# Row edges computed as corrections on a few columns, beside a convolution that now runs over all 1024 columns

## The chip, the cores and the metric

The kernel runs on one core of one Trainium2 chip. Five engines work side by side, each with its own instruction stream: TensorE (PE in the profile, its weight loads PEld), VectorE (DVE), ScalarE (ACT), GpSimd (POOL) and SyncE (SP), which here issues nearly all transfers. The metric is the device time of one execution in microseconds; lower is better. Three runs of the kernel before took 474.04, 475.82 and 476.01 us, so the median is 475.82 us. A run of the profiler on the same kernel has a span of 475.5 us from its first to its last instruction.

## The reference

Four linear layers along a row of 1024 columns with 64 channels, for 128 samples, and a residual. Each layer scales its input channels by a style vector of the sample and its output channels by a normalising factor; the kernel folds the four layers into one convolution per sample wherever the row's ends do not matter.

```python
def _layer(x, style, w, b, mw, mb, typ):
    s = style @ mw.T + mb
    weight = SCALE * w * s[:, None, :, None]
    demod = lax.rsqrt(jnp.sum(weight * weight, axis=(2, 3)) + EPS)
    weight = weight * demod[:, :, None, None]
    if typ == 'same':
        out = jax.vmap(_conv_same)(x, weight) + b[None, :, None]
    elif typ == 'upsample':
        out = jax.vmap(_conv_up)(x, weight.transpose(0, 2, 1, 3)) + b[None, :, None]
        out = _blur(out, 2.0 * blur_k, (1, 1))
    elif typ == 'downsample':
        xb = _blur(x, blur_k, (2, 2))
        out = jax.vmap(_conv_down)(xb, weight) + b[None, :, None]
    return out
out = x                                   # (128, 64, 1024) float32
for i, typ in enumerate(('same', 'upsample', 'same', 'downsample')):
    out = _layer(out, style, weights[i], biases[i], mod_w[i], mod_b[i], typ)
x = x + out
```

Near the two ends of a row the zero padding of each single layer counts, so the one folded convolution is not what the four layers give there; this concerns the first three and the last three columns.

## The kernel before

**Tiling.** The 128 samples are 32 quads of four (`NQ` = 32, index `q`). The partitions hold 64 channels of one sample above 64 channels of another, and a quad has two such pairs in the free dimension. A row is split into three phase planes (every third column). `NB` = 340 is the number of output columns that the folded convolution makes per plane, 1020 in all, of which the host keeps 1018; the first and last three columns of the output come from elsewhere.

**One product.** For a quad the convolution is done as five products (`conv0` to `conv4`, all through `product`, L792) of summed input planes (tiles `T04`, `T12`, `T3`, made by `in04`, `in1`, `in2`, `in3` from `X` and from the half sums `G`) with summed weights. A product is three tap groups times four 64x64 quadrants of the array, twelve calls of `nc.tensor.matmul`, each with `NB` moving columns; float32 leaves two records for each call, so a product shows as 24 records of L803. `conv3`, `conv1`, `conv2`, `conv0` write the PSUM tile `psA` of their quad (pool `ps_conv`, two buffers, so quad `q+1` takes the buffer of quad `q-1`); `conv4` writes the single tile `Y`. VectorE carries partial results between them (`sum1`, `sum2`), ScalarE scales the three finished planes into the tile `o` (`outputs`, pool `opool`, two buffers), and SP stores them.

**The chain of weights.** In the same loop the folded weights of later quads are made by small matmuls: `stage1` (L428), `stage2` (L506, L589; ScalarE copies its result out as `R`, GpSimd adds two sums in `r_sums`, L638), `stage3` (L621). `share` (L506 into `psA`) puts part of stage 2 into the unused columns of `psA` from `NB + 4` on.

**A turn.** `turn_of(q)` (L1483) writes the instructions of all engines in order by hand for q = 4 to 28; `early_turn` does it for q = 0 to 3 and a straight piece of code from L1560 on for the last three quads. The order of the parts on TensorE in a turn is: stage 2 of quad q+2, `conv2(q)`, the first part of stage 3 (which opens the `psA` buffer for quad q+1), `conv4(q)`, the rest of stage 3, `conv3(q+1)`, stage 1, `conv0(q)`, more of stage 1, `share`, the slot (below), `conv1(q+1)`.

**The row ends.** `x_ends` brings eight columns of each end of each row (one zero column and seven of x) into `Xe`. They go through the four layers exactly, for all 128 samples at once, in five slots: `ends0` in turn 10, the two halves of `ends1` in turns 14 and 15, `ends2` in turn 19 (all four into `Y`) and `ends3` in turn 28 (into a tile of its own, `psE`). Each slot is three taps times four quadrants, 12 calls or 24 records of L1044 (`ends_matmul`), directly ahead of `conv1`. Upper and lower array rows hold the two row ends, and a matmul has 64 samples times up to eight columns. After a slot VectorE scales the result (`rest0` to `rest3`); the steps between slots (`setup_x`, `setup0`, `add0`, `setup1`, `rest1_bias`, `rest1_edges`, `setup3`, `add2`, `blur_side`) lie one by one in other turns through the table `SIDE`, in VectorE's order just behind `in_g2`. GpSimd zeroes the borders of the tiles in `zeros` (turn 6). At the end `rest3_bias` (L1158) adds bias and x and issues two stores of 96 KB on SP.

Of the kernel before, what the change touches and what calls it, by code (L numbers as in the profile page):

```python
# [54 lines left out]
C = 64  # L55
K = 3
# [7 lines left out]
def kernel(  # L64
# [74 lines left out]
    Xs = [const.tile([P, 2, NXC], F32, name=f"X{i}") for i in range(NX)]  # L139
# [24 lines left out]
    Xe = const.tile([P, B, 8], F32, name="Xe")  # L164
# [9 lines left out]
    NB = 340  # L174
# [578 lines left out]
    def g_tile(q):  # L753
        if q not in Gs:
            Gs[q] = gpool.tile([P, 2, 3 * PL], F32, tag="G", name=f"G{q}")
        return Xs[q % NX], Gs[q]
# [136 lines left out]
    WIDE = 6  # L893
    ends_ps = {}

    def slot(matmuls, n, ps, wide=WIDE):
        matmuls(ps)
        ends_ps[0] = ps, max(n, wide)

    def last(i, n, j):  # L900
        ps, w = ends_ps[0]
        return ps[i][:, : n * w].rearrange("c (b j) -> c b j", b=n)[:, :, :j]


# [81 lines left out]
    Xm = const.tile([P, B, 8], F32, name="Xm")  # L986
    Xs0 = [Xm[:, :HB], Xm[:, HB:]]
    a0, c0, a2, c2 = (const.tile([P, HB], F32, name=n) for n in ("a0", "c0", "a2", "c2"))
    g1 = const.tile([P, 6, C], F32, name="g1")

    Ye = [const.tile([P, HB, 8], F32, name=f"Ye{s}") for s in range(2)]
    Ue = [const.tile([P, HB, 11], F32, name=f"Ue{s}") for s in range(2)]
    Ve = [const.tile([P, HB, 12], F32, name=f"Ve{s}") for s in range(2)]
    Oe = const.tile([P, B, 3], F32, name="Oe")

    def zeros():
        for t in Ye:
            nc_g.memset(t[:, :, 0:1], 0.0)
            nc_g.memset(t[:, :, 7:8], 0.0)
        for t in Ue:  # L1000
            nc_g.memset(t[:, :, 0:1], 0.0)
            nc_g.memset(t[:, :, 10:11], 0.0)
        for t in Ve:
            nc_g.memset(t[:, :, 0:2], 0.0)
            nc_g.memset(t[:, :, 10:12], 0.0)
        nc_g.memset(g1, 0.0)

    def spread(t, n):

        return t[:, :, None].to_broadcast([P, t.shape[1], n])  # L1010
# [7 lines left out]
    def setup_x(h):  # L1018
        bs = slice(h * HB, (h + 1) * HB)
        nc_v.tensor_tensor(Xm[:, bs], Xe[:, bs], spread(sc[:, 0, bs], 8), op=ALU.mult)  # L1020

    def setup0():

        for rows, bs in ((T, slice(0, HB)), (Bo, slice(HB, B))):
            nc_v.tensor_mul(a0[rows], dm[rows, 1, bs], dm[rows, 0, bs])
            nc_v.tensor_copy(c0[rows], c0f[rows, bs])
# [4 lines left out]
    def setup3():  # L1031
        for rows, bs in ((T, slice(0, HB)), (Bo, slice(HB, B))):
            nc_v.tensor_copy(a2[rows], Da[rows, bs])
            nc_v.tensor_copy(c2[rows], c2f[rows, bs])

    def ends_matmul(ps, n, taps, weight, moving, wide=WIDE):
        for i in reversed(range(taps)):
            first = i == taps - 1
            w = max(n, wide)
            m = w if first else n  # L1040
            for r, rows in enumerate(HALF):
                for c, cols in enumerate(HALF):
                    dst = ps[r][cols, : HB * w].rearrange("c (b j) -> c b j", j=w)
                    nc.tensor.matmul(  # L1044
                        dst[:, :, :m],
                        weight(i, r, c)[rows],
                        moving(i, r, c, m)[rows],
                        start=first,
                        stop=(i == 0),
                        skip_group_check=True,  # L1050
                    )

    def ends0(ps):

        ends_matmul(
# [11 lines left out]

    def ends1(part):

        n = 5 - part  # L1070


        def weight(i, r, c):
# [648 lines left out]
```

## Time and profile before

| What | Value |
|---|---|
| Runs of the kernel | 474.04, 475.82, 476.01 us |
| Span of the profiled execution | 475.5 us |
| PE busy / records | 469.7 us (99%) / 11932 |
| VectorE busy | 417.3 us (88%) |
| ScalarE busy | 312.0 us (66%) |
| GpSimd busy | 165.8 us (35%) |
| DMA | 70.71 MB, mean 149 GB/s |
| VectorE's waits at `sum2` for TensorE (L712 behind L803) | 26.9 us in 26 waits |
| Mean granted TensorE clock | 0.998 |

How to read it: the page gives for each engine the time in which at least one of its instructions ran. Records of TensorE overlap (four quadrants run side by side, and a record goes on for some time after the next has begun), so the busy time of a group of matmuls is not what it costs. What a group costs is read from the timeline, as the difference between the start of its first record and the start of the first record of the next group. In a line of the timeline the columns are start and length in microseconds, the engine, the line of the kernel, the operation, the tiles written and read, the shape and the number of records; idle time before it, with what ended it, stands in brackets.

### The profile page before, as it was taken

The page shows a single profiled execution, that of the slowest core. Times are in us where ns is not written, and L with a number is a line of the kernel's source. Part 1 is how long each engine was busy: PE and PEld are TensorE (multiplying, and loading weights), DVE is VectorE, ACT ScalarE, POOL GpSimd, SP SyncE. Part 2 cuts the span into 40 slices and gives each one's busy share as a digit, 9 for nine tenths or more (in the row PEclk, how much of TensorE's full clock was granted, in tenths as well). Part 3 has the DMA queues.
Part 4 walks back from the last instruction along what each step waited for, and adds up shares of the span by engine and source line. Part 5 has one row for each costly group of instructions (what it writes and reads, how often), then busy time and mean ns, then how long its engine had stood idle before and what let it go on. Part 6 is the DMA issues. An engine that isn't in the chain of part 4 may idle for free.

```text
span 475.5 us, 26771 instructions
## 1 busy us (share of the span) xinstructions
PE 469.7 (99%) x11932; PEld 349.5 (74%) x11932; DVE 417.3 (88%) x694; ACT 312.0 (66%) x711; POOL 165.8 (35%) x200
## 2 busy tenths in 40 slices
PE   9999999999999999999999999999999999999996
PEld 6987788777678876677776677766788787876653
DVE  3889998879989998899979899979998999999896
ACT  4565657577766676766667666667666777766464
POOL 3634033664444342233432233422333423243200
PEclk9999999999999999999999999999999999999999
DMA  5237456535445554345544454543555544455225
GB/s 176 71 115 224 150 151 180 152 113 177 139 145 166 166 166 136 123 150 169 163 150 126 130 168 152 178 124 121 152 164 169 164 145 147 148 152 161 80 91 193
DMA packets 52707, 70.71 MB, mean 149 GB/s; under 512 B 6000, under 2 KB 50672, under 8 KB 52592
## 3 DMA queue, kind: packets, MB, share of 16 engines
q1 hardware_dynamic: 52368, 68.78, 46.3%
q8 instruction: 93, 1.52, 1.4%
q10 hardware_dynamic: 224, 0.22, 0.1%
q14 instruction: 22, 0.18, 0.1%
HBM read 35.36 MB, written 33.62 MB: 145 GB/s over the span
## 4 chain that ended last, share of the span: by engine, by line
PE 99%; DVE 0%; ACT 0%; issue 0%
PE psA L803 47%; PE Y L803 12%; PE psR L506 9%; PE psW L621 7%; PE psA L621 7%; PE psS L428 6%; PE psR L589 5%; PE psA L506 2%; PE Y L1044 2%; PE Y L183 1%; PE Y L379 1%; PE psM L220 0%; PE psE L1044 0%; PE Y L255 0%; DVE o L882 0%; PE psM L255 0%
## 5 line engine op out<-in xcount | busy, mean ns | idle before, releaser
L803 PE MATMUL psA<-T,H 64*64 64x340 f32 x2304 | 185.9, 446 | 0.0
L803 PEld LDWEIGHTS psA<-T,H 64*64 64x64 f32 x2304 | 90.7, 133 | 46.9 <-issue 2.5
L712 DVE SCALAR_TENSOR_TENSOR G<-X 128x1376 f32<-128x1376 f32 (+2 forms) x65 | 78.0, 1206 | 0.2
L776 POOL TENSOR_TENSOR T<-G 128x684 f32<-128x684 f32 x28 | 46.3, 1652 | 73.7 <-DVE G L712 73.7
L484 POOL TENSOR_TENSOR S<-S 128x128 f32<-128x128 f32 x28 | 21.6, 772 | 139.7 <-ACT S L399 139.6
L399 ACT ACTIVATE R<-psR,tC 128x448 f32<-128x448 f32 x63 | 36.6, 631 | 43.6 <-PE psR L506 25.8
L803 PE MATMUL psA<-T,Wf 64*64 64x340 f32 x768 | 63.7, 446 | 0.0
L803 PE MATMUL Y<-T,Wf 64*64 64x340 f32 x768 | 62.4, 451 | 0.0
L712 DVE SCALAR_TENSOR_TENSOR Y<-m,psA 128x340 f32<-128x340 f32 x62 | 32.0, 516 | 28.2 <-PE psA L803 26.9
L399 ACT ACTIVATE psW<-psA 128x128 f32<-128x128 f32 x100 | 19.3, 268 | 49.1 <-PE psA L621 45.0
L790 DVE TENSOR_TENSOR T<-G 128x1368 f32<-128x1368 f32 (+1 forms) x33 | 50.8, 1541 | 0.0
L399 ACT ACTIVATE Wf<-psW,t 128x256 f32<-128x256 f32 (+2 forms) x76 | 32.7, 480 | 26.7 <-PE psW L621 26.4
L761 DVE TENSOR_TENSOR T<-X 128x684 f32<-128x684 f32 x32 | 47.7, 1492 | 0.0
L506 PE MATMUL psR<-S,E 64*64 64x64 f32 (+1 forms) x1472 | 46.8, 237 | 0.0
L781 POOL TENSOR_TENSOR T<-G 128x684 f32<-128x684 f32 x28 | 46.5, 1660 | 0.0
L428 PEld LDWEIGHTS psS<-wd,w2n 64*64 64x64 f32 x1120 | 35.1, 133 | 12.9 <-issue 0.3
L506 PEld LDWEIGHTS psR<-S,E 64*64 64x64 f32 x1472 | 39.5, 134 | 4.9 <-ACT psR L529 0.2
L803 PEld LDWEIGHTS Y<-T,Wf 64*64 64x64 f32 x768 | 30.3, 132 | 16.8
L803 PEld LDWEIGHTS psA<-T,Wf 64*64 64x64 f32 x768 | 29.8, 133 | 14.5
L880 ACT ACTIVATE o<-psA,tb,td 128x340 f32<-128x340 f32 x63 | 37.1, 648 | 5.0 <-PE psA L803 2.8
L880 ACT ACTIVATE o<-y,tb,td 128x340 f32<-128x340 f32 x62 | 38.5, 678 | 0.0
L880 ACT ACTIVATE o<-Y,tb,td 128x340 f32<-128x340 f32 x62 | 36.1, 639 | 2.8 <-PE Y L803 2.0
(180 smaller groups left out, 840.4 us busy)
## 6 DMA issues: line engine op xcount, KB each, us to landing
out<-o SPq DMA_DIRECT2D x191, 170.0 KB, 2.6
X<-in_x SPq DMA_DIRECT2D x150, 172.0 KB, 3.4
X<-in_x SPq DMA_DIRECT2D x14, 516.0 KB, 5.0
par<-in_params SPq DMA_DIRECT2D x3, 192.0 KB, 3.8
Xe<-in_x_ends SPq DMA_DIRECT2D x1, 512.0 KB, 4.5
out<-Oe SPq DMA_DIRECT2D x2, 96.0 KB, 2.1
out<-o ACTq DMA_DIRECT2D x1, 170.0 KB, 2.8
par<-in_params SPq DMA_DIRECT2D x1, 160.0 KB, 2.7
```

The costliest lines, as they stand in the source:

```text
L399: nc_a.activation(dst, src, AF.Copy, scale=f)
L428: nc.tensor.matmul(ps[r][cols, at * C : (at + n) * C], weight[rows], wd[c if r == 0 else 1 - c][rows, taps], start=first, stop=last, skip_ ...
L506: nc.tensor.matmul(dst[r][cols], weight[rows], st[c if r == 0 else 1 - c][rows, slots, :], start=False, stop=last, skip_group_check=True,)
L589: nc.tensor.matmul(ps[r][cols, lo * C : (lo + m) * C], E[rows, e + 2, :], src[rows, a, :], start=(n == 0), stop=(n == 8), skip_group_check ...
L621: nc.tensor.matmul(dst[r][cols], weight[rows], t[rows, c, slots, :], start=first, stop=last, skip_group_check=True,)
L712: nc_v.scalar_tensor_tensor(out, x, f, y, op0=ALU.mult, op1=op)
L761: nc_v.tensor_sub(t[:, pairs, 0, :NJ], plane(X, 3, pairs), plane(X, 1, pairs))
L776: eng.tensor_add(t[:, :, 0, :NJ], plane(g, 2), plane(g, 1))
L781: eng.tensor_sub(t[:, :, 1, :NJ], plane(g, 2), plane(g, 1))
L790: nc_v.tensor_sub(t[:, pairs, :, :NJ], both(a, PL), both(b, 1))
L803: nc.tensor.matmul(ps[s][cols, :NB], w, Ts[q, tag][rows, c, i, g : g + NB], start=(g == 0 and (m == 3 or alone)), stop=(g == K - 1), skip_ ...
L880: nc_a.activation(dst, src, AF.Identity, bias=add, scale=d3)
```

## The change

The folded convolution now covers all 1024 columns: `NB` goes from 340 to 342, the planes hold four zero columns ahead of the row instead of one, their length `PL` stays 344, and `X` and `G` get eight spare columns behind each pair's planes (zeroed once by GpSimd), since `in_g01` and `in_g2` now read and write one column past the third plane. What the folded convolution gives for the three outermost columns at each end is wrong by a linear correction. Only that correction goes through the layers, on three columns of x at an end instead of eight: `Xe` has 3 columns per row end, and the intermediate tiles `Ye`, `Ue`, `Ve`, `We` have 4, 6, 6 and 6. The right end is stored mirrored, so both ends use one column order, and the two ends stand in the output partitions' halves while the two samples of a pair stand in the array rows' halves.

The matmuls of a layer are now a list of single taps with their source and destination columns. `ends0` has 3 of them (with 3, 2 and 1 columns), `ends1` 6 in one piece (2, 2, 2, 2, 1, 1), `ends2` 4 (5, 4, 2, 1) and `ends3` 4 (2, 1, 2, 2), each four quadrants with 64 row pairs. There are four slots instead of five. A slot of the table stands in the turn after its number (turns 11, 15, 19 and 27), between stage 2 and `conv2(q)`, and writes the `psA` tile of quad q-1, whose outputs are done; the VectorE step `rest` of the slot stands behind `r_sums` and ahead of `sum2`. `ends3` moves from turn 28 to turn 27.

The correction `Oe` is subtracted from the outputs that ScalarE has already written: for every quad GpSimd picks the three outermost columns of both ends out of the tile `o` with two small copies (`gather`, `correct`) into `Oc`; once `Oe` is there, VectorE subtracts it for the first 27 quads in one step (`correct_all`, turn 28) and SP stores them; quads 27 to 30 are subtracted by GpSimd while they are picked, and quad 31 by VectorE behind the last two outputs, with a second store at the very end. The small tables that the ends need are made by GpSimd in turns 8 to 10 (`end_tables`).

```diff
-    Xs = [const.tile([P, 2, NXC], F32, name=f"X{i}") for i in range(NX)]
+    Xs = [const.tile([P, 2, NXC + 8], F32, name=f"X{i}") for i in range(NX)]
+    for t in Xs:
+        nc_g.memset(t[:, :, NXC:], 0.0)
...
-    NB = 340
+    NB = 342
...
-            sum_of(g[:, pairs, PL:], X[:, pairs, : 2 * PL], 0.5, X[:, pairs, PL:], ALU.subtract)
+            n = 2 * PL + 1
+            a, b = X[:, pairs, :n], X[:, pairs, PL : PL + n]
+            sum_of(g[:, pairs, PL : PL + n], a, 0.5, b, ALU.subtract)
...
+    Xm = const.tile([P, 2, HB, K], F32, name="Xm")
+    Ye = const.tile([P, 2, HB, 4], F32, name="Ye")
+    Ue = const.tile([P, 2, HB, 6], F32, name="Ue")
+    We = const.tile([P, 2, HB, 6], F32, name="We")
+    Oc = const.tile([P, HB, 2, K], F32, name="Oc")
...
+    def ends_matmul(ps, n, moving, plan):
+        for i, (weight, src, dst) in enumerate(plan):
             for r, rows in enumerate(HALF):
                 for c, cols in enumerate(HALF):
+                    out_ = ps[r][cols, : HB * n].rearrange("c (b j) -> c b j", j=n)
+                    d = dst(r) if callable(dst) else dst
                     nc.tensor.matmul(
+                        out_[:, :, d],
+                        weight(r, c)[rows],
+                        moving[rows, c, :, src],
+                        start=(i == 0),
...
     def ends0(ps):
+                (w[2], slice(0, 3), slice(0, 3)),
+                (w[1], slice(0, 2), slice(1, 3)),
+                (w[0], slice(0, 1), slice(2, 3)),
...
+    def ends1(ps):
+                (g[0], slice(2, 4), slice(1, 6, 4)),
+                (g[2], slice(1, 3), slice(1, 6, 4)),
+                (g[1], slice(1, 3), slice(0, 3, 2)),
+                (g[4], slice(0, 2), slice(3, 6, 2)),
+                (g[3], slice(1, 2), slice(2, 3)),
+                (g[5], slice(0, 1), slice(4, 5)),
...
+    def rest1(t):
+        nc_v.tensor_tensor(Ue, in_psum(t, 6), spread(both_ends(a1h), 6), op=ALU.mult)
...
+    def ends2(ps):
+                (w[0], slice(0, 5), slice(0, 5)),
+                (w[1], slice(1, 5), slice(0, 4)),
+                (w[2], slice(2, 5, 2), slice(0, 3, 2)),
+                (w[2], slice(5, 6), slice(1, 2)),
...
+    def ends3(ps):
+                (w[0], slice(0, 3, 2), lambda r: slice(0, 2 + r, 1 + r)),
+                (w[0], slice(4, 5), lambda r: slice(2 - r, 3 - r)),
+                (w[1], slice(1, 4, 2), lambda r: slice(0, 2 + r, 1 + r)),
+                (w[2], slice(2, 5, 2), lambda r: slice(0, 2 + r, 1 + r)),
...
+    def correct(q, planes, eng=nc_g):
+        src, b = edges(q, planes)
+        at = slice(b, b + 2)
+        if q < LATER_ENDS:
+            eng.tensor_copy(Oc[:, at, :, planes], src)
+        else:
+            eng.tensor_sub(Oc[:, at, :, planes], src, Oe[:, at, :, planes])
+
+    def gather(q):
+        for planes in (slice(1, K), slice(0, 1)):
+            correct(q, planes)
+
+    def correct_all(n):
+        nc_v.tensor_sub(Oc[:, : 2 * n], Oc[:, : 2 * n], Oe[:, : 2 * n])
+        store_ends(0, n)
...
-    SLOTS = {
-        10: (ends0, 6, rest0),
-        14: (ends1(0), 5, lambda: rest1(0)),
-        15: (ends1(1), 4, lambda: rest1(1)),
-        19: (ends2, 8, rest2),
-    }
+    SLOTS = {10: (ends0, rest0), 14: (ends1, rest1), 18: (ends2, rest2), 26: (ends3, rest3)}
...
+            if q - 1 in SLOTS:
+                SLOTS[q - 1][0](banks(q - 1))
             conv2(q)
             r_sums(c, nc_g)
+            if q - 1 in SLOTS:
+                SLOTS[q - 1][1](A[q - 1])
             sum2(q)
...
         outputs(q, 0)
-        if q in SLOTS:
-            matmuls, width, rest = SLOTS[q]
-            slot(matmuls, width, Y_banks)
-            rest()
-        if s == NQ:
-            slot(ends3, 3, unit(ps_w, "psE"), 3)
-            rest3()
         conv1(n, *((2,) if entry else range(K)))
...
         in3(c)
-        side(LATE, q)
+        gather(q - 1)
...
         in1(c, nc_g)
...
-    rest3_bias(0)
-    rest3_bias(1)
+    correct(q, slice(1, K))
...
         store(q, i, slice(2, K))
+    correct(q, slice(1, K), nc_v)
     conv0(q, *range(K))
     for i, (eng, queue) in enumerate(zip(BOTH, (nc_a, nc.sync))):
         output(q, 0, i, eng)
         store(q, i, slice(0, 1), queue)
+    correct(q, slice(0, 1), nc_v)
+    store_ends(LATER_ENDS, NQ)
...
-    NBL = 170
-    PL = 2 * NBL + 4
-    pad = np.pad(x, ((0, 0), (0, 0), (1, 3 * PL - 1 - L)))
+    NBL = 171
+    PL = 2 * NBL + 2
+    pad = np.pad(x, ((0, 0), (0, 0), (4, 3 * PL - 4 - L)))
```

More of the change, by code (lines that the diff above doesn't have):

```diff
@@ L1584 @@
     outputs(q, 0)
+    for i in range(2):
+        for planes in (slice(1, K), slice(0, 1)):
+            correct(q - i, planes)
     conv2(n)
```

264 lines of the change are left out of this document (116 added, 148 removed).

## The prediction

> **What bounds the kernel.** I read the page first: the busy shares, the slices and the chain of work that ended last.
>
> ```profile
> span 475.5 us, 26771 instructions
> ...
> PE 469.7 (99%) x11932; PEld 349.5 (74%) x11932; DVE 417.3 (88%) x694; ACT 312.0 (66%) x711; POOL 165.8 (35%) x200
> ...
> PE 99%; DVE 0%; ACT 0%; issue 0%
> ```
>
> TensorE is busy for 99% of the span and the chain runs through it from end to end. But a busy TensorE may still be slower than its columns allow, so next I looked in its timeline at what a group costs from its start to the start of the next one.
>
> ```profile
> 252.06 1.90 PE L803 MATMUL psA<-T,H 64*64 64x340 f32 x24
> 253.78 0.73 PE L428 MATMUL psS<-wd,w2n 64*64 64x128 f32 x24
> ```
>
> A product of 24 records takes 253.78 - 252.06 = 1.72 us, that is 71.7 ns a record and 71.7 / 340 = 0.211 ns a column. The same price holds for the dense slots of the row ends below. So the kernel is bound by the number of columns that stream through TensorE, and other engines matter only where TensorE waits for them. The change is therefore first a count of columns.
>
> **Two more columns in every product.** The groups of line 803 by shape give the number of records.
>
> ```profile
> L803 PE MATMUL psA<-T,H 64*64 64x340 f32 x2304 | 185.9, 446 | 0.0
> L803 PE MATMUL psA<-T,Wf 64*64 64x340 f32 x768 | 63.7, 446 | 0.0
> L803 PE MATMUL Y<-T,Wf 64*64 64x340 f32 x768 | 62.4, 451 | 0.0
> ```
>
> These are 3840 records, each with 2 columns more: 3840 x 2 x 0.211 ns = 1.62 us added, all on the path.
>
> **The old slots, removed.** TensorE's timeline around the five slots; what counts is again the start of the slot to the start of the product behind it.
>
> ```profile
> 183.76 2.12 PE L1044 MATMUL Y<-Xm,par 64*64 64x384 f32 x24
> 185.70 0.74 PE L803 MATMUL psA<-T,H 64*64 64x340 f32 x6
> ...
> 241.06 1.92 PE L1044 MATMUL Y<-Ye,g 64*64 64x384 f32 x24
> 242.79 0.76 PE L803 MATMUL psA<-T,H 64*64 64x340 f32 x8
> ...
> 256.63 1.81 PE L1044 MATMUL Y<-Ye,g 64*64 64x384 f32 x24
> 258.25 0.76 PE L803 MATMUL psA<-T,H 64*64 64x340 f32 x8
> ...
> 313.75 2.78 PE L1044 MATMUL Y<-Ue,par 64*64 64x512 f32 x24
> 316.35 1.03 PE L803 MATMUL psA<-T,H 64*64 64x340 f32 x12
> ...
> 440.35 1.58 PE L1044 MATMUL psE<-Ue,par 64*64 64x192 f32 x24
> 441.75 1.04 PE L803 MATMUL psA<-T,H 64*64 64x340 f32 x12
> ```
>
> They cost 1.94 + 1.73 + 1.62 + 2.60 + 1.40 = 9.29 us, and all of it goes. Three of them have one shape throughout and give prices: `ends0` 1.94 us for 24 x 384 columns, 0.2105 ns a column; `ends2` 2.60 us for 24 x 512, 0.2116 ns; `ends3` 1.40 us for 24 x 192, 0.304 ns. `ends3` is the only one that reads every second column of its tile, in runs of three; a stepped read costs 1.44 times a dense one here.
>
> **The new slots, added.** A tap with m columns is 8 records of 64 x m columns. `ends0` has 3 + 2 + 1 = 6 columns a row pair, `ends1` 10, `ends2` 12, `ends3` 7: 35, or 35 x 512 = 17,920 columns. Dense in the old sense (long runs on both sides) are the first two taps of `ends0` and of `ends2`, 14 columns or 7168. The other 21, or 10,752, take one column of a row or every second or fourth one, reading, writing or both. No row shows such a short run. Lower bound: all at the dense price, 17,920 x 0.2105 = 3.77 us. Upper bound: it is not the columns that cost but the 64 runs, so that each of the 34 waves of four records takes what one of `ends3`'s six took, 1.40 / 6 = 0.233 us: 7.93 us. I take the dense price for the 7168 and the stepped price of 0.304 ns for the 10,752, since `ends3` is the nearest row: 1.51 + 3.27 = 4.78 us (0.70, 1.56, 1.44 and 1.09 us by slot).
>
> [...]
>
> **Where the slots stand.** A slot now lies between stage 2 and `conv2`, and its result must leave PSUM before the first part of stage 3 opens that buffer. The whole timeline of a turn without a slot shows the neighbours.
>
> ```profile
> 273.80 0.65 ACT L880 ACTIVATE o<-psA,tb,td 128x340 f32<-128x340 f32 x1
> ...
> 274.57 1.65 POOL L776 TENSOR_TENSOR T<-G 128x684 f32<-128x684 f32 x1 [2.81 <-DVE G L712]
> ...
> 275.10 1.85 DVE L761 TENSOR_TENSOR T<-X 128x684 f32<-128x684 f32 x1
> ...
> 275.77 1.90 PE L803 MATMUL psA<-T,H 64*64 64x340 f32 x24
> 276.06 1.16 ACT L399 ACTIVATE R<-psR,tC 128x448 f32<-128x448 f32 x2 [0.72 <-PE psR L506]
> ...
> 277.30 0.73 POOL L638 TENSOR_TENSOR R<-R 128x256 f32<-128x256 f32 x1 [1.08 <-ACT R L399]
> 277.48 0.94 PE L621 MATMUL psA<-R,w0s 64*64 64x192 f32 x24
> 277.73 1.07 DVE L712 SCALAR_TENSOR_TENSOR Y<-m,psA 128x340 f32<-128x340 f32 x2 [0.78 <-PE psA L803]
> ...
> 278.85 0.52 PE L803 MATMUL Y<-T,Wf 64*64 64x340 f32 x4
> ```
>
> The buffer's last output by ScalarE ends at 274.45, and the slot would begin at 275.77, so it does not wait. `conv2` then takes 277.48 - 275.77 = 1.71 us, and in that time VectorE must do `rest`. VectorE is free from 276.95 on and idles 0.78 us before `sum2`.
>
> ```profile
> L1119 DVE TENSOR_TENSOR Ve<-Y,a 128x512 f32<-128x512 f32 x2 | 1.3, 688 | 0.8 <-PE Y L1044 0.8
> L1062 DVE TENSOR_TENSOR Ye<-Y,a 128x384 f32<-128x384 f32 x2 | 1.0, 550 | 0.0
> ...
> L712 DVE SCALAR_TENSOR_TENSOR Y<-m,psA 128x340 f32<-128x340 f32 x62 | 32.0, 516 | 28.2 <-PE psA L803 26.9
> ...
> L712 DVE SCALAR_TENSOR_TENSOR y<-psA,m 128x680 f32<-128x680 f32 x31 | 26.7, 862 | 6.1 <-PE psA L803 4.7 <-PE Y L964 1.3
> ```
>
> Reads from PSUM grow by (688 - 550) / 128 = 1.08 ns a column, so the four `rest` steps (384, 768, 640 and twice 192 columns) take about 0.55, 0.96, 0.83 and 0.55 us, the largest 0.75 us less than `conv2`. Cost nothing, by the cover of `conv2`; without it up to their sum, 2.9 us. Behind a late `rest` on VectorE stands `sum2`, and `conv4` waits for that with no slack: `sum2` ends at 278.80 and `conv4` starts at 278.85. For that reason the two added columns of `sum2` do count: (862 - 516) / 340 = 1.02 ns a column, two columns in 62 records, 0.13 us. `r_sums` and the copies of `R` only gain cover.
>
> **GpSimd, VectorE's small steps, transfers.** A `gather` is two very small operations a quad, and it stands behind the sum of stage 1 and ahead of `in1` (L776).
>
> ```profile
> L335 POOL TENSOR_TENSOR t<-dm,var 64x8 f32<-64x8 f32 x4 | 0.8, 203 | 0.2
> ...
> POOL S L484 <- ACT S L399: 139.6, 26, 11.8
> ```
>
> At 0.2 us each they take 0.4 us of the 2.81 us in which GpSimd waits there for VectorE; if that idle time were gone, the 1.08 us ahead of `r_sums` would still be there before TensorE noticed. Nor do ScalarE's next writes to the tile wait: it has two buffers, and the copies are done a turn ahead. `end_tables` falls into the 139.6 / 26 = 5.4 us in which GpSimd waits for stage 1 in each turn. VectorE's steps between slots get fewer and narrower; that gains nothing while TensorE sets the pace, nor do the smaller load and the dropped stores. In turn 28 `correct_all`'s store holds up SP until VectorE has passed; behind it wait only stores whose outputs ScalarE has not yet written.
>
> **The end.** The last two rows of the timeline and two rows of the transfers:
>
> ```profile
> 471.06 0.63 DVE L882 TENSOR_SCALAR o<-psA,td,tb 128x340 f32<-128x340 f32 x1 [0.28 <-PE psA L803]
> 471.66 0.39 ACTq L885 DMA_DIRECT2D out<-o  x1
> 471.72 0.33 SPq L885 DMA_DIRECT2D out<-o  x1
> ...
> out<-Oe SPq DMA_DIRECT2D x2, 96.0 KB, 2.1
> ...
> out<-o ACTq DMA_DIRECT2D x1, 170.0 KB, 2.8
> ```
>
> ScalarE's last store lands at 471.66 + 2.8 = 474.5. The new last step, a VectorE subtraction of a few columns (about 0.2 us by the GpSimd row above, far as it is), ends near 471.9 and fits beside the issue of SP's store, which ends at 472.05. The store behind it lands at 472.1 + 2.1 = 474.2 if it goes like the old one, at 474.9 if it goes like the large one: between nothing and 0.4 us. I take 0.1, nearer to the small transfer.
>
> **The sum.** 1.62 - 9.29 + 4.78 + 0.13 + 0.1 = -2.66 us against the profiled 475.5 us. The median of the runs is 0.3 us above that span, so the forecast is 475.8 - 2.7 = 473.1 us.
>
> **Rivals.** (1) Short runs cost nothing extra: 3.77 us for the slots, 472.1 us. For it: the third old slot with runs of four of six is near the dense price; against: `ends3`. (2) A price per run: 7.93 us, 476.3 us, no change. For it: `ends3`'s wave of 64 runs; against: 64-run slots with longer runs show only their columns. (3) A new wait takes the place of the slots removed: stage 3 stands until `rest` has left the buffer, in four turns, because VectorE is behind: 473.1 + 2.9 = 476.0 us. Against it: VectorE's waits at `sum2`, 26.9 us in all. (4) The other side: every scattered column, not every run, costs a wave of 0.233 us in each of its two passes. Then the 21 scattered columns take 21 x 0.467 = 9.8 us, with the dense ones 11.3 us, 6.5 more than forecast, and the kernel takes 479.6 us. It decides in `ends1` and `ends3`; slower than before from 7.4 us of slots on, by over 0.5% from 9.8 us on. Against it: `ends3` itself has such columns, three in a run, and paid a third of that for each.
>
> **Chances.** Forecast 0.48, with a range of its own from 472.4 to 474.3; (1) 0.20, (2) 0.14, (3) 0.10, (4) 0.08. Half a per cent, about what a measurement here can tell from no change, is 2.4 us, so faster means under 473.4 us: (1) and 0.28 of the forecast's 0.48 (473.1 lies just under that line), 0.48. No change: the other 0.20, (2) and (3), 0.44. Slower: (4), 0.08. The range reaches from 0.5 us below (1) to (2): 471.6 to 476.4 us.
>
> **What would show it.** In the changed profile: products of 24 records in 1.73 us; slots of 0.7, 1.6, 1.4 and 1.1 us from start to start, which tell the forecast from (1), (2) and (4); no idle time of TensorE or its weight loads ahead of stage 3 in the four slot turns, against (3); `in1` still waiting for VectorE; the last transfer landing within 3.3 us of the last output. The forecast is wrong if the slots together are over 6 us, or if turns without a slot grow by more than the 0.05 us of their five products.

## The result, and the profile after

The changed kernel takes 495.41 us (median of 4 runs, 493.04 to 499.9) against 475.04 us before: a ratio of 1.0441, 95% interval 1.0384 to 1.0498. (With a fourth run, of 474.27 us, the median of the kernel before is 475.04 in place of 475.82 us.) The forecast was 473.1 us. One run of the experiment i2 below, 502.89 us, counts as slow, over 1.5% above the fastest of its kernel, and is left out of its time. The profiled execution is the run of 499.9 us. From its page, the lines that answer to those of before:

```profile
span 498.1 us, 26874 instructions
...
PE 475.7 (96%) x11948; PEld 359.4 (72%) x11948; DVE 414.4 (83%) x676; ACT 311.2 (62%) x711; POOL 178.4 (36%) x266
...
PEclk9999999999999999999999999999999998998997
...
q1 hardware_dynamic: 52496, 68.65, 49.5%
...
PE 91%; issue 3%; DVE 3%; ACT 1%; another core or an unknown queue 1%; POOLq 0%; POOL 0%; DVEq 0%; ACTq 0%
...
L623 PE MATMUL psA<-R,w0s 64*64 64x128 f32 (+2 forms) x1000 | 37.6, 263 | 7.3 <-issue 7.2
```

TensorE is still by far the busiest, but it is no longer full: 22.4 us of the span are idle, where before 5.8 us were. The last line tells where: in the products of stage 3 with `R` (L623), idle 7.3 us, and nearly all of it put down to "issue", that is, to nothing that the profile shows. No late operand is on record there. TensorE's waits, of the changed kernel (line, what it waited for, us in total, times, longest):

```profile
PE psA L623 <- issue: 10.2, 9, 1.9
PE psA L807 <- issue: 1.2, 2, 0.6
```

and of the kernel before:

```profile
PE psA L621 <- issue: 0.2, 1, 0.2
```

So the same wait occurs in both, once before and eleven times at these two lines here (a stall is such a stop of TensorE). The timeline of TensorE in one of the worst turns:

```profile
412.75 1.04 PE L807 MATMUL psA<-T,H 64*64 64x342 f32 x12
413.62 0.92 PE L623 MATMUL psA<-R,w0s 64*64 64x192 f32 x18
415.58 0.36 PE L623 MATMUL psA<-R,w0s 64*64 64x128 f32 x3 [1.05 <-issue]
...
415.84 0.31 PE L623 MATMUL psA<-R,par 64*64 64x64 f32 x4
417.28 0.27 PE L623 MATMUL psA<-R,par 64*64 64x64 f32 x1 [1.13 <-issue]
...
417.94 2.12 PE L807 MATMUL Y<-T,Wf 64*64 64x342 f32 x12
```

The whole of stage 3 between `conv2` and `conv4` takes 417.94 - 413.62 = 4.32 us here. The same products took 278.85 - 277.48 = 1.37 us before, by the rows of the prediction.

What stands at these places is seen when all records of TensorE and of its weight loads are counted in order of their start, 24,025 of them (11,948 matmuls, 11,948 weight loads, 129 others). The profile's page lists a queue "instruction" that moved 94 packets with 1.54 MB, 16,384 bytes each. 24,025 / 94 = 255.6, and the packets keep step with the records: the n-th one ends when between 256 n - 60 and 256 n + 165 records have begun. So 256 records are called a block here, by the author's estimate one packet of TensorE's instructions. The stalls of over half a microsecond, with their place in the block, and the end of the last such packet ahead of them:

```
stall, us from span's start   lost us   record   place in block   last packet's end
136.20 -> 137.39              1.13       6337    193              135.54
165.50 -> 166.82              1.28       7873    193              163.95
325.78 -> 326.36              0.53      16578    194              324.97
354.19 -> 355.08              0.84      18114    194              352.73
383.41 -> 384.76              1.30      19650    194              381.80
398.56 -> 400.64              2.03      20418    194              396.90
415.93 -> 417.28              1.29      21186    194              412.75
432.93 -> 433.93              0.72      21954    194              430.91
```

Eight of the eleven stand at place 193 or 194, 62 or 63 records ahead of a block's end; the other three (0.78, 1.21 and 2.09 us) stand at 166, 170 and 255. In the kernel before the one stall of the loop is at place 193 too (350.87 us, 0.36 us). A turn without a slot has 768 matmuls and weight loads, three times 256, and about four other records, so such a place moves by only a few records from turn to turn: in all eight rows it lies in stage 3 or at the end of `conv2` ahead of it. This fits a wait for the next block of instructions. It does not show the transfer itself as late: in all eight rows the last packet had ended 0.7 to 3.2 us before the stall began, and none is under way in a stall. What lies between the packet's end and TensorE's going on is not in the trace.

The transfers themselves are slower. From the share of queue q1, one packet took on average 0.495 x 16 x 498.1 us / 52,496 = 75 ns. The row of the kernel before,

```profile
q1 hardware_dynamic: 52368, 68.78, 46.3%
```

gives 0.463 x 16 x 475.5 / 52,368 = 67 ns. By size, a packet of a store takes 66 ns on average against 62 before, one of a load of `X` 93 against 77; the longest took 2.2 and 2.9 us against 0.3 and 1.0. And the stores land late. SyncE's waits for them in the loop (L889) and at the end (L1726), of the changed kernel:

```profile
SPq L889 <- DMA out<-o: 8.3, 11, 1.6
...
SPq L1726 <- DMA out<-o: 5.8, 2, 3.8
```

and of the kernel before, where it waits only at the end:

```profile
SPq L1713 <- DMA out<-o: 2.4, 3, 1.3
```

From the end of TensorE's last product to the end of the span it is 8.7 us against 4.5 before. So the output is slower to land and the loads are slower; the stalls come with them.

### The profile page after: what moved, and what is told of

Same layout as the page of the kernel before. It is cut to its first block, busy times and chain, and to the rows that moved or that the text cites. A ratio compares the mean times of both kernels' runs of the same rounds, so it can differ in the third digit from the quotient of the medians.

```text
span 498.1 us, 26874 instructions
## 1 busy us (share of the span) xinstructions
PE 475.7 (96%) x11948; PEld 359.4 (72%) x11948; DVE 414.4 (83%) x676; ACT 311.2 (62%) x711; POOL 178.4 (36%) x266
## 3 DMA queue, kind: packets, MB, share of 16 engines
q1 hardware_dynamic: 52496, 68.65, 49.5%
q8 instruction: 94, 1.54, 1.5%
## 4 chain that ended last, share of the span: by engine, by line
PE 91%; issue 3%; DVE 3%; ACT 1%; another core or an unknown queue 1%; POOLq 0%; POOL 0%; DVEq 0%; ACTq 0%
PE psA L807 43%; PE Y L807 11%; PE psR L508 9%; PE psW L623 7%; PE psA L623 7%; PE psS L430 5%; PE psR L591 5%; PE psA L508 2%; PE psA L1042 1%; DVE Y L714 1%; PE Y L185 1%; ACT o L884 0%; DVE T L763 0%; DVE o L1616 0%
## 5 line engine op out<-in xcount | busy, mean ns | idle before, releaser
L807 PE MATMUL psA<-T,H 64*64 64x342 f32 x2304 | 190.6, 449 | 1.3 <-issue 1.2
L807 PEld LDWEIGHTS psA<-T,H 64*64 64x64 f32 x2304 | 95.0, 134 | 47.0 <-issue 5.2
L714 DVE SCALAR_TENSOR_TENSOR G<-X 128x1378 f32<-128x1378 f32 (+2 forms) x65 | 78.4, 1211 | 0.2
L780 POOL TENSOR_TENSOR T<-G 128x688 f32<-128x688 f32 x28 | 46.4, 1657 | 69.2 <-DVE G L714 69.2
L807 PE MATMUL Y<-T,Wf 64*64 64x342 f32 x768 | 66.0, 468 | 0.3 <-DVE Y L714 0.2
L807 PE MATMUL psA<-T,Wf 64*64 64x342 f32 x768 | 64.5, 448 | 0.0
L794 DVE TENSOR_TENSOR T<-G 128x1376 f32<-128x1376 f32 (+1 forms) x33 | 51.0, 1547 | 0.0
L763 DVE TENSOR_TENSOR T<-X 128x688 f32<-128x688 f32 x32 | 51.0, 1594 | 0.0
L807 PEld LDWEIGHTS Y<-T,Wf 64*64 64x64 f32 x768 | 34.6, 138 | 17.1 <-DVE Y L714 1.4
L785 POOL TENSOR_TENSOR T<-G 128x688 f32<-128x688 f32 x28 | 46.4, 1658 | 0.0
L623 PE MATMUL psA<-R,w0s 64*64 64x128 f32 (+2 forms) x1000 | 37.6, 263 | 7.3 <-issue 7.2
L623 PEld LDWEIGHTS psA<-R,w0s 64*64 64x64 f32 x1000 | 34.0, 133 | 14.5 <-issue 9.0
L807 PEld LDWEIGHTS psA<-T,Wf 64*64 64x64 f32 x768 | 31.2, 133 | 13.8 <-ACT m L1645 0.2
L884 ACT ACTIVATE o<-psA,tb,td 128x342 f32<-128x342 f32 x63 | 37.2, 651 | 5.1 <-PE psA L807 5.1
```

The source lines that it names most:

```text
L623: nc.tensor.matmul(dst[r][cols], weight[rows], t[rows, c, slots, :], start=first, stop=last, skip_group_check=True,)
L714: nc_v.scalar_tensor_tensor(out, x, f, y, op0=ALU.mult, op1=op)
L763: nc_v.tensor_sub(t[:, pairs, 0, :NJ], plane(X, 3, pairs), plane(X, 1, pairs))
L780: eng.tensor_add(t[:, :, 0, :NJ], plane(g, 2), plane(g, 1))
L785: eng.tensor_sub(t[:, :, 1, :NJ], plane(g, 2), plane(g, 1))
L794: nc_v.tensor_sub(t[:, pairs, :, :NJ], both(a, PL), both(b, 1))
```

## The experiments

Each time stands beside runs of the kernel before on the same chip (medians from 475.04 to 475.43 us).

**Which part of the change.** Three candidates: the new layout of the output (theory L), the gathers and subtractions (G), or chance. The changed kernel once more:

> The changed kernel as it is, on the chip of the next three runs. Theory F: TensorE starves for its own instructions; its stalls of 0.5 to 2 us carry no wait, stand in the trace 62 records before the end of a block of 256, and vary from run to run. Then again 490 to 500 us, with stalls in the same place of a turn but not in the same turns. Theory N (a chance disturbance of the first chip): 472 to 476 us.

496.63 us (1.0467, 1.0451 to 1.0483). It was no chance.

The kernel before, with only the output's planes and the widths of `X` and `G` as the change has them:

```diff
+    OP = 342
...
-            out[q, :, s, planes.start * NB : planes.stop * NB],
+            out[q, :, s, planes.start * OP : planes.start * OP + NB],
```

> The kernel before, with 340 columns as it was, but with the memory layout of the change: planes of the output and of the tile o 342 columns apart, X and G eight columns wider. Theory L (the layout slows the transfers, and the instruction blocks come late behind them): 485 to 497 us, X packets as slow as in the changed kernel (mean over 85 ns against 76). Rival G (the gathers on GpSimd or the moved slots do it): 474 to 477 us.

485.07 us (1.022, 1.0193 to 1.0248): without any of the new row ends, half of the loss is there. Much of it is not in TensorE's stream: in the profiled execution (481.9 us against 475.5) 2.8 us are lost up to TensorE's last product and 3.6 us behind it, where 8.1 us pass in place of 4.5.

The changed kernel with planes 344 elements apart, in memory and in the tile `o` (`OP = 344`; only 342 of each are written):

> The changed kernel with the planes of the output and of the tile o 344 columns apart, so that every piece starts at a multiple of 32 bytes. Theory L: 472 to 477 us, without the stalls of TensorE that carry no wait. Rival G: 490 to 498 us, as it was.

475.73 us (1.0012, 0.9993 to 1.0032): all of the loss is gone. TensorE's timeline of stage 3 in the turn that took 4.32 us above:

```profile
402.08 0.94 PE L624 MATMUL psA<-R,w0s 64*64 64x192 f32 x24
402.85 0.29 PE L624 MATMUL psA<-R,par 64*64 64x64 f32 x8
402.96 0.41 PE L624 MATMUL psA<-R,w0s 64*64 64x64 f32 x16
403.19 0.40 PE L624 MATMUL psA<-R,par 64*64 64x128 f32 x8
403.46 0.81 PE L808 MATMUL Y<-T,Wf 64*64 64x342 f32 x8
```

1.38 us, without a wait.

The changed kernel without gathers and subtractions; `Oe` is stored in place of `Oc`, so the edges lack their convolution over all rows:

```diff
     def correct(q, planes, eng=nc_g):
+        return
...
-        nc_v.tensor_sub(Oc[:, : 2 * n], Oc[:, : 2 * n], Oe[:, : 2 * n])
```

> The changed kernel without the gathers, the subtractions and their semaphores; the small correction itself is stored in place of the corrected edge columns. Theory G: 472 to 477 us. Theory L: 490 to 498 us, as it was.

495.01 us (1.0445, 1.039 to 1.0501): theory G falls.

**Memory or the tile, and which alignment.** A piece is what a store writes of one row: one plane's 340 or 342 columns, 1360 or 1368 bytes. Planes 344 apart in memory alone, then in the tile alone:

> The changed kernel with only the output in memory padded: its planes stand 344 elements apart (each piece of 1368 bytes begins at a multiple of 32 bytes), while the tile o on the chip keeps planes 342 apart. If the start of a piece in memory is what costs (theory M), this run takes about 476 us like the run with both padded (475.73), the stalls of TensorE at places 193 and 194 of a 256-instruction block are gone and the last store lands within about 1.3 us. If the start on the chip costs (theory S), it stays at 493 to 498 us.

> The changed kernel with only the tile o padded: planes 344 apart on the chip, 342 apart in memory as in the change. Theory M: 493 to 498 us, stalls as in the changed kernel, the last wait for a store 3 to 4 us. Theory S: about 476 us. If both ends count for part of it, this run and the one with memory padded lie between, 480 to 490 us each.

475.61 us (1.0005, 0.999 to 1.002) and 494.38 us (1.0408, 1.0352 to 1.0465). It is the place in memory. Two runs then asked how far alignment helps:

> The kernel before with its output planes 344 elements apart in memory and in the tile o, instead of 340 (1360 bytes: starts at multiples of 16 bytes, not always of 32). Theory M with a threshold at 16 bytes: no difference from before, 474 to 476 us. Theory M with a cost that goes on falling to 32 bytes: faster, 470 to 474 us, and then the change itself, layout aside, is slower than its kernel before by as much.

> The changed kernel with planes 352 elements apart in memory (1408 bytes, every piece begins at a multiple of 64 bytes) and 344 in the tile o. If 32 bytes are enough: 475 to 476.5 us as with 344. If a piece should begin at 64 bytes: 470 to 474 us, with fewer stalls left than the two located ones (0.3 and 0.5 us) of the run with 344.

475.12 us (0.9989, 0.9977 to 1.0001): the kernel before gains nothing. 473.99 us (0.9972, 0.996 to 0.9984) for the change with planes 352 apart: a version faster than both kernels, by 0.3%. The same layout in the kernel before:

> The kernel before with planes 352 apart in memory (starts at multiples of 64 bytes) and 344 in the tile o. If 64 bytes is worth the same here as in the change (475.6 to 474.0 us from 344 to 352): 473.5 to 474 us, and then the row edges as corrections bring nothing by themselves. If before gains nothing from it: 475 us, and the change is 1.1 us faster at equal layout.

474.8 us (0.9997, 0.9984 to 1.001). So with planes 352 apart the change is worth 474.8 - 473.99 = 0.8 us (on two chips). With planes 344 apart, both on one chip, it is 475.61 - 475.12 = 0.5 us slower (f1 against f3; e3, with the tile padded too, took 475.73). At equal layout the change is therefore worth little either way, and its sign is not settled.

**Not the start of a piece.** Planes 346 apart begin at 8-byte places again, with 16 bytes free between them:

> The changed kernel with planes 346 apart in memory: every piece again begins at an odd multiple of 8 bytes or less aligned than 32 (1384 bytes a plane), but 16 bytes lie free between two pieces, so that no two pieces touch. If the cost comes from the start of a piece (theory M): 490 to 498 us, as with 342. If it comes from two stores that share a line of memory at their seam: about 475 us, as with 344.

474.71 us (0.9987, 0.9975 to 0.9998). The theory that a piece's start has to be aligned (M), which had explained the runs so far, falls. What the change altered together with the seams, where two planes meet without a free byte, is the distance between two rows of the output: 6 x 340 x 4 = 8160 bytes before, 6 x 342 x 4 = 8208 in the change. Only that distance is altered here:

```diff
-            out[q, :, s, planes.start * NB : planes.stop * NB],
+            out[q, :, s * 1026 + planes.start * NB : s * 1026 + planes.stop * NB],
...
-    for i, shape in enumerate(([B // 4, 2 * C, 2, 6 * NBL], [2 * C, B * 3])):
+    for i, shape in enumerate(([B // 4, 2 * C, 2064], [2 * C, B * 3])):
```

> The change with its planes of 342 side by side as they are (seams at 8-byte places, pairs 1026 elements apart), and only each row of the output 2064 elements long in place of 2052: rows 8256 bytes apart in place of 8208. Theory R (the distance between rows, 8192 + 16): about 475 us, no stalls at places 193 and 194. Theory S (seams and 8-byte places): 490 to 498 us, unchanged.

475.22 us (0.9991, 0.9981 to 1.0002). 48 unused bytes at the end of each row take the whole loss away, with planes side by side and seams where the change has them. From the page of this run and its waits, TensorE's busy time, the packets and SyncE's last wait for a store:

```profile
PE 466.1 (98%) x11948; PEld 344.0 (73%) x11948; DVE 416.1 (88%) x676; ACT 311.6 (66%) x711; POOL 182.9 (39%) x266
...
q1 hardware_dynamic: 52496, 68.65, 45.0%
...
SPq L1726 <- DMA out<-o: 1.9, 3, 1.3
```

TensorE has the same 24,025 records in this run as in the change, so the two can be compared record by record. The profiled change is 24.4 us longer (498.1 against 473.7): it falls 20.7 us behind up to the last product and 3.7 us more after it. Half of the 20.7, 10.4 us, is lost ahead of the sixteen records at places 193 to 208 of their blocks; in e1 it is 10.8 of 18.2.

The mirror of it, the kernel before with rows of 8208 and of 8192 bytes (2052 and 2048 elements, the second pair at element 1024):

> The kernel before, planes of 340 side by side as they are (every piece begins at a multiple of 16 bytes), only its rows 2052 elements long: 8208 bytes apart, as in the change. Theory R: 482 to 497 us, with stalls of TensorE at the border of blocks and a last wait for a store of 3 to 4 us. Theory S: 475 us.

> The kernel before with rows of 2048 elements, 8192 bytes apart. Theory R, if what counts is how little the rows of one store move against 8192: slower than the same with 8208, 495 to 530 us. If it is the odd 16 bytes: about 475 us. Theory S: 475 us.

477.61 us (1.0052, 1.0037 to 1.0067) and 475.23 us (0.9999, 0.9986 to 1.0011). 8208 alone costs the kernel before 2.4 us, not the 7 to 22 expected; 8192 costs nothing, so nearness to 8192 is not it. Two runs for what was left, 8224 bytes (2056 elements), and 8208 bytes with 136 rows for each part of the output in place of 128:

```diff
-            out[q, :, s, planes.start * NB : planes.stop * NB],
+            out[q, :P, s, planes.start * NB : planes.stop * NB],
...
-    for i, shape in enumerate(([B // 4, 2 * C, 2, 6 * NBL], [2 * C, B * 3])):
+    for i, shape in enumerate(([B // 4, 2 * C + 8, 2, 6 * NBL], [2 * C, B * 3])):
```

> The change with rows of 2056 elements, 8224 bytes apart in place of 8208, pieces at 8-byte places and planes side by side as they are. If only rows that are an odd multiple of 16 bytes apart hurt together with 8-byte places: about 475 us. If what counts is how near the rows' distance lies to 8192: between, 477 to 490 us.

> The change with its rows of 8208 bytes as they are, but 136 rows in place of 128 for each part of the output (four examples), of which the last 8 are never written: the distance between rows stays, the step from one part to the next grows from 1,050,624 to 1,116,288 bytes. Theory R (distance between the rows of one store): 490 to 498 us, unchanged. Theory D (where the parts lie): another time, down to 475 us.

475.45 us (1.0009, 0.9995 to 1.0023) and 498.74 us (1.0471, 1.0412 to 1.053). 16 bytes more in a row are enough, and moving the parts does not cure it. All layouts side by side:

```
row, bytes   planes begin at   free bytes between planes   kernel           us
8160         16 bytes          none                        before           475.0 to 475.4
8192         16 bytes          none                        before (h3)      475.23
8208         16 bytes          none                        before (h2)      477.61
8208          8 bytes          8                           before (e2)      485.07
8208          8 bytes          none                        after            495.41, 496.63
8208          8 bytes          none                        after (f2, i2)   494.38, 498.74
8224          8 bytes          none                        after (i1)       475.45
8256          8 bytes          none                        after (h1)       475.22
8256         32 bytes         16                           before (f3)      475.12
8256         32 bytes          8                           after (e3, f1)   475.73, 475.61
8304          8 bytes         16                           after (g1)       474.71
8448         64 bytes         40                           after (f4)       473.99
8448         64 bytes         48                           before (g3)      474.8
```

Every kernel with rows of 8208 bytes is slower, and no other one is. In the kernel before it costs 2.4 us with planes at 16-byte places and 10 us with planes at 8-byte places; in the change, with no byte free between planes, 19 to 24 us. Between 10 and 20 both the free bytes and the kernel differ, so which of them counts is not separated. Why 8208 does it, the runs do not tell. The first rule in the expectation of i1 stays open too: of the distances tried, all multiples of 16, only 8208 and 8304 are odd ones, and with 8304 (g1) 16 bytes lay free between planes.

**Are the stalls those of a block of instructions?** (Theory F.) Small products of zeros ahead of the first quad move every later instruction within its block.

```diff
     zeros_to_y(2, 96, False)
+    for _ in range(16):
+        zeros_to_y(2, 32, False)
```

> The change with its own 342 planes, and 64 small products of zeros (128 records on TensorE, 64 x 32 columns each) added before the first pair, so that every later instruction stands half a 256-instruction block further on. They add at most 2 us at the start. Theory F (TensorE waits for its next block of instructions, whose fetch is late while the stores keep memory busy): the stalls stand at places 193 and 194 of a block again and so at other lines than before, not inside the products of stage 3 (L623) with R, and their sum changes; where the boundary falls into a stretch that has more slack, the time drops by several us. Rival (something at the line itself, such as a read of psA or R that is not shown): the stalls stay at L623 with R, at places 65 and 66, and the time stays at 493 to 498 us.

520.63 us (1.0941, 1.0883 to 1.0999). The 64 products are 256 records (24,281 against 24,025), twice what the expectation says and a whole block, so every instruction kept its place in its block, and the run cannot tell the theories apart. That the same program with one more block in front is 25 us slower still was not expected and stays unexplained; its trace shows more of the same (TensorE idle for 35.0 us against 22.4, granted clock 0.975 against 0.988), not why. Half as many (`range(8)`), 128 records:

> The change as it is, with 32 small products of zeros before the first pair, 128 records and so half a block of instructions. Theory F (the next block of instructions comes late): the stalls stand at places 193 and 194 of a block again, which are now other instructions of the turn, not the ones of stage 3 with R at which they stood; the time is another than 495 us, lower if the new border has more slack behind it. Rival (something at the line itself): stalls stay at stage 3 with R, 495 to 498 us and the added products' 1 to 2 us.

488.45 us (1.0271, 1.0246 to 1.0295). The output is as slow as ever (SyncE's longest last wait for a store is 3.1 us), but the stalls have moved to other instructions:

```profile
441.85 0.79 PE L807 MATMUL Y<-T,Wf 64*64 64x342 f32 x2
443.31 1.09 PE L807 MATMUL Y<-T,Wf 64*64 64x342 f32 x12 [0.67 <-issue]
```

This is `conv4`, and the record stands at place 193 of its block. Of the five stalls over 0.45 us in the loop three stand at 193 or 194: two at L807 and one at L623 with `psW`, none at `psA<-R`, where seven of the eight above stood. Of the other two, one (0.8 us, L623) is a wait for VectorE's `rest3`. The added products cost time (the first `conv4` starts at 32.98 us against 30.03), and yet the kernel is 7 to 8 us faster than the change, and TensorE is idle for 12.9 us of its span against 22.4. So these stalls go with places 193 and 194 of the blocks and not with a line. How much of the 7 to 8 us comes from where these places fall is not shown: g2 left them where they were and changed the time by more.

**The turn that stayed long.** With the layout cured (f4), one stall of 1.1 us is left. It stands between the `conv4` of quad 28 and that of quad 29 (the expectation's turn 29), where VectorE also does `correct_all`. The subtraction was given to GpSimd:

```diff
-        nc_v.tensor_sub(Oc[:, : 2 * n], Oc[:, : 2 * n], Oe[:, : 2 * n])
+        nc_g.tensor_sub(Oc[:, : 2 * n], Oc[:, : 2 * n], Oe[:, : 2 * n])
```

> The change with planes 352 apart in memory, and the one subtraction over all earlier pairs (correct_all, 128x324, 0.49 us on VectorE in turn 28) given to GpSimd, which idles about 7 us there. If that subtraction is what pushes VectorE's next work into GpSimd's additions (T<-G 3.03 us in place of 1.58) and makes TensorE wait 1.26 us for Y in turn 29: that turn falls from 14.75 to 13.6 to 13.9 us and the time to 472.8 to 473.2 us. If not: 474 us and the turn stays at 14.75.

474.97 us (0.9989, 0.9973 to 1.0005), and that stretch takes 14.94 us: a miss, the subtraction is not the cause.

## Why the prediction was wrong

The step that failed is the one on transfers, put at nothing without a reason: it asked only how many there are ("nor do the smaller load and the dropped stores") and had no term for the output's own, without a look at where its rows lie. `NB = 342` makes a row of the output 8208 bytes long in place of 8160, and that is 495.4 - 475.2 = 20 us (the change against h1). None of the four rivals was about transfers, so the range could not hold it either. That the row distance does it is shown by h1, which alters nothing else. From there to TensorE the chain is in part argued: stores land late and loads are slower (measured), TensorE stops at one place of a block (193 or 194 in eight of eleven stalls of the change, and at other lines in h4, three of five), and between the two stands a fetch of instructions that comes late, which no trace shows: the author read it from their coming and going together in the runs. In the kernel before such a place cost 0.36 us, once in the loop; here it cost up to 2.0 us.

The other steps can be judged by f4, in which nearly nothing of this is left. Time from the `conv4` of a quad to that of the next, in us, under the number of the second (the old slots lie in 11, 15, 16, 20 and 29, the new ones in 11, 15, 19 and 27):

```
quad                   10     11     15     16     19     20     27     29
before, 352 (g3)       13.84  15.78  15.56  15.49  13.95  16.44  13.90  14.82
change                 14.02  16.23  15.91  13.90  15.44  14.50  17.96  14.90
change, 352 (f4)       13.90  14.62  15.89  13.90  15.44  13.90  15.15  14.75
```

*The two columns* were right: 13.90 against 13.84 us without a slot.

*The new slots* were right in size. TensorE's timeline of f4, each slot from its start to the product behind it:

```profile
185.61 0.90 PE L1043 MATMUL psA<-Xm,par 64*64 64x192 f32 x24
186.33 1.91 PE L808 MATMUL psA<-T,H 64*64 64x342 f32 x24
...
241.92 1.08 PE L1043 MATMUL psA<-Ye,g 64*64 64x128 f32 x28
243.20 0.68 PE L1043 MATMUL psA<-Ye,g 64*64 64x128 f32 x16 [0.20 <-issue]
243.70 0.47 PE L808 MATMUL psA<-T,H 64*64 64x342 f32 x1
...
299.51 1.72 PE L1043 MATMUL psA<-Ue,par 64*64 64x320 f32 x32
301.03 1.35 PE L808 MATMUL psA<-T,H 64*64 64x342 f32 x16
...
412.23 1.44 PE L1043 MATMUL psA<-We,par 64*64 64x128 f32 x32
413.48 1.34 PE L808 MATMUL psA<-T,H 64*64 64x342 f32 x16
```

0.72, 1.52 and 1.25 us for `ends0`, `ends2` and `ends3`, against 0.70, 1.44 and 1.09. `ends1` makes its stretch 15.89 - 13.90 = 1.99 us longer, against 1.56, but place 193 of a block falls into it (at 251.22 us in the trace of the change), and TensorE is idle there for 0.20 us. In h4, where the slot stands 128 records further on and the place falls outside it:

```profile
249.72 0.29 PE L1042 MATMUL psA<-Ye,g 64*64 64x128 f32 x2
...
249.75 1.59 PE L1042 MATMUL psA<-Ye,g 64*64 64x128 f32 x46
251.08 1.99 PE L807 MATMUL psA<-T,H 64*64 64x342 f32 x24
```

251.08 - 249.72 = 1.36 us: less than forecast, and a quarter over the dense 5120 x 0.2105 = 1.08 us. With this 1.36 the four slots are 4.85 us against 4.78 forecast; with the 1.99 of f4, 5.5. That the sums agree so well is in part luck: `ends1` is 0.20 us under its price and the other three 0.26 over theirs. Rivals (1), (2) and (4), with 3.77, 7.93 and 11.3 us, are out. (The third old slot, which spoke for (1), had cost 1.62 us for 24 records with 7168 columns in all, 0.226 ns a column, 7% over the dense price.)

*The old slots* were wrong in one term. Four of them went with what they cost, but the fifth, 1.40 us ahead of quad 29's `conv4`, brought 0.08: 14.82 to 14.75 us. It had lain beside VectorE's work. The last rows of that stretch before, with planes 352 apart (g3), and then of f4:

```profile
444.02 1.90 PE L804 MATMUL psA<-T,H 64*64 64x340 f32 x24
...
446.50 0.94 PE L622 MATMUL psW<-R,w0s 64*64 64x128 f32 x24
447.26 1.90 PE L804 MATMUL Y<-T,Wf 64*64 64x340 f32 x24
```

```profile
440.70 1.90 PE L808 MATMUL psA<-T,H 64*64 64x342 f32 x24
...
443.19 0.94 PE L624 MATMUL psW<-R,w0s 64*64 64x128 f32 x24
445.23 1.09 PE L808 MATMUL Y<-T,Wf 64*64 64x342 f32 x12 [1.10 <-DVE Y L715]
```

From the last products of stage 3 to `conv4` it was 0.76 us and is now 2.04. VectorE's timeline in f4 shows what is late:

```profile
439.38 1.86 DVE L764 TENSOR_TENSOR T<-X 128x688 f32<-128x688 f32 x1
441.16 3.03 DVE L795 TENSOR_TENSOR T<-G 128x1376 f32<-128x1376 f32 x1
444.11 1.06 DVE L715 SCALAR_TENSOR_TENSOR Y<-m,psA 128x342 f32<-128x342 f32 x2
```

`sum2` waits behind an addition of 3.03 us. In the same stretch of the kernel before, VectorE and then GpSimd:

```profile
443.79 0.87 DVE L712 SCALAR_TENSOR_TENSOR y<-psA,m 128x680 f32<-128x680 f32 x1 [1.08 <-PE psA L803]
...
446.24 1.57 DVE L790 TENSOR_TENSOR T<-G 128x1368 f32<-128x1368 f32 x1
```

```profile
443.95 1.64 POOL L781 TENSOR_TENSOR T<-G 128x684 f32<-128x684 f32 x1
```

VectorE stood 1.08 us waiting for TensorE, and its addition began after GpSimd's had ended (445.59) and took 1.57 us. In f4 the two overlap, and both take longer; GpSimd's there:

```profile
440.46 2.28 POOL L786 TENSOR_TENSOR T<-G 128x688 f32<-128x688 f32 x1
```

The prediction asked what lies beside other work of all that the change adds, and not of what it removes. Of VectorE's 33 additions at this line in f4 this is the only one that overlaps an addition of GpSimd's, and the only one over 1.7 us; in g4, where the subtraction is gone from VectorE, the same one overlaps and takes 3.03 us again. That the overlap is the whole cause was not tried by moving one of the two.

*What was costed at nothing* otherwise held: TensorE has no wait for `rest` in f4, against rival (3), and one of 0.8 us in h4; leaving out the gathers changes nothing that shows beside the spread of e4's runs (493.4 to 499.0 us); and from the last `conv4` to the end the change takes 7.8 us against 7.6.

Summed with what was measured, against g3: columns and `sum2` +1.75 (the forecast's own terms), four old slots -(1.94 + 1.72 + 1.65 + 2.60) = -7.91, the fifth -0.08, new slots +5.50, end +0.2: -0.5 us, where the medians say -0.8. The forecast's -2.66 lacked 1.3 us in the fifth slot and 0.7 in the new ones, 0.63 of it between the `ends1` of f4 and that of h4; both are small beside the 20. That f4's 473.99 us lies in the forecast's own range is luck: the sum behind it was off by 2 us.

## What to carry to other kernels

When a change alters the size of something that lives in memory, the distance between its rows belongs into the sum: try the same kernel with padded rows before judging the change's arithmetic (16 or 48 bytes more took away 20 us here). Idle time of TensorE under "issue" is worth a count of the records ahead of it: here eight of eleven stalls kept to place 193 or 194 of every 256 records, and the loss came and went with the layout of the output in memory; that the supply of instructions lies between the two is the author's reading. And ask of every removed piece of work what ran beside it: it may have cost nothing (the fifth old slot, 1.40 us long, brought 0.08).

## What the runs showed that was not expected

- Rows of 8208 bytes cost 2.4 us and more (20 us in the change), rows of 8192, 8224, 8256, 8304 and 8448 bytes nothing, with the same pieces of 1360 or 1368 bytes.
- At place 193 or 194 of a block of 256 records, 62 or 63 ahead of its end, TensorE stopped eight times for 0.5 to 2.0 us; in the kernel before it did so once in the loop, for 0.36 us.
- One block more in front of the loop made the changed kernel 25 us slower (g2), half a block 7 us faster (h4). Why a whole block changes the time is open.
- After two of the stalls TensorE's granted clock fell to 0.50 and 0.51, from 417.6 to 421.0 and from 451.7 to 455.1 us. The `conv4` in each of them took 3.26 and 3.06 us to the start of the next products, against 1.77 at 255.03 us, where the clock was 1.00. If all work there slowed with the clock, these 6.8 us hold the work of 3.4, so by estimate about 3.4 us of the profiled run's loss are clock. (Its mean is 0.988 over the span, against 1.000 in f4.)
